# Cross attention in split fp32 on one core: one direct fp32 result unit in batch one in place of two, the softmax sums of batch one folded by accumulating transfers, its order of work written anew, and ten warming products

## The chip, the cores and the metric

The kernel runs on one core of a Trainium2 chip. The metric is device time in microseconds from the start of the program to its end; the median of several runs is compared. A core has five engines that each take their instructions in order: PE (matrix products), ACT (ScalarE), DVE (VectorE), POOL (GpSimd) and SP (SyncE, which here only issues transfers). They wait for each other through semaphores. PE writes to PSUM, ACT and DVE read it; everything else lies in SBUF, 128 partitions wide.

## The reference

Eight batches of cross attention, B = 8, C1 = C2 = 512 channels, N = 1024 positions, D = 64:

```python
q = jnp.einsum('bcn,dc->bnd', x1, Wq) + bq
k = jnp.einsum('bcn,dc->bdn', x2, Wk) + bk[:, None]
v = jnp.einsum('bcn,dc->bdn', x2, Wv) + bv[:, None]
attn = jax.nn.softmax(jnp.einsum('bnd,bdm->bnm', q, k), axis=2)
attn_out = jnp.einsum('bcm,bnm->bcn', v, attn)
return attn_out + x1
```

All of it is fp32, and the inputs are laid out on the host so that channels or positions stand on partitions.

## The kernel before, in words

**Products.** A product of two fp32 operands can be done directly, as PE's fp32 matmul, or in three passes of a faster type (fp32r) on operands that were split. Of an operand a, h is a rounded (`wh`, `xh`, `vh`, `H`), l is the rest (`wl`, `xl`, `vl`, `l`) and d = h - T l, with T = 4096 (`wd`, `xd`, `vd`, `d`). The passes with h and l go to one PSUM bank, X, the pass with d to another, Y, and (T + 1) X - Y gives the product, up to scale and sign. The splitting is work for ACT (h) and DVE (l and d).

**Stages of a batch.** `Q` and `K` project x1 and x2 with the small weights (eight direct products each, 16 rows in the trace); `qe`, `ke` evacuate them on ACT, `qd`, `kc` copy each half to the other 64 partitions by DMA from SP's queue, `qr`, `kr` round them on ACT and `ql`, `kl` make the low halves on DVE. V is made for eight blocks j of 128 positions: `VX.j` and `VY.j` (split, 8 and 4 products), after `sy.j` has put the bias as a seed into Y's bank; `cy.j` on ACT takes Y out and `jn.j` on DVE joins X and Y to `v4`, two blocks to a pair p; `vh.p`, `vl.p`, `vd.p` split the pair again. In batch one the blocks 0 to 2 are direct products instead (`VF.j.c`, four each, joined by `jf.j`). The scores are `S.h.i`: half h (512 queries) and key block i, two products each (with kh and kl against qa), copied out of PSUM by `Sc.h.i` on ACT.

**Softmax and result.** The queries stand in quarters Q of 256 and units u of 128. `F.Q` takes the maximum of a quarter over the key blocks on DVE (four operations), `T.Q` takes it over partitions on POOL, `L.u` subtracts it on DVE, `E.u` is the exponential on ACT, `H.u`, `l.u`, `d.u` split the unit. The result of a unit is `R.u.m`, m = 0 to 7: three split products for each pair of key block and unit, 24 for a unit. In batch one, units 0 and 1 are direct products instead (`RF.u.m`, 8 for a unit, from the unsplit exponentials and v4); they need no H, l and d, and `of.u` evacuates them. Elsewhere `oy.u` on ACT takes Y out with its share of the denominator, and `o.u` on DVE joins it with X. `oa.u` adds x1 by an accumulating DMA from HBM in POOL's queue, `st.u` stores.

**The denominators.** `es.Q` copies half of a quarter's exponentials on ACT, `a1.Q` adds the other half by an accumulating DMA (512 KB) in POOL's queue, `a2.Q` and `a3.Q` fold four columns to two and two to one on DVE (`join`), `tot.Q` sums over partitions on POOL, `few.Q` turns the row into a column with two tiny copies on SP, `rec.Q` is the reciprocal on DVE, and `r2.Q` scales it on ACT. `of`, `oy` and `o` need it.

**Order.** Every engine's order is the order of the words in three lists, written out by hand: `FIRST` for batch one, `MIDDLE` for the six batches between, `LAST`. A word with + belongs to the next batch: its loads (`ldx1`, `ldx2`), Q, K and first scores run inside this one. A scheduler adds the waits and nothing else. PSUM has eight banks: three X, three Y and two for scores ("sc"), handed out in turn; batch one's scores with odd i take a Y bank, and Q and K use the score banks too. Before all that, `begin` issues the first loads and lets PE multiply zeros, nine times, in banks of Y.

Of the kernel before, what the change touches and what calls it, by code (L numbers as in the profile page):

```python
# [27 lines left out]


FIRST = """  # L30
wh.0 VF.0.0 VF.1.0 wl.0 VF.0.1 VF.1.1 wd.0 w4.0 wh.1 VF.0.2 VF.1.2 wl.1 VF.0.3 wd.1 w4.1 ldx2.0 lwq VF.2.0
xh.1 VF.2.1 xl.1 VF.2.2 xd.1 VF.2.3 ldx2.1 lsd xh.2 xh.3 bv xl.2 xl.3 jf.0 jf.2 xd.2 xd.3 sy.3 sy.4 sy.5 K ke
VF.1.3 jf.1 vh.0 vl.0 vd.0 ldx1.0 VY.3 cy.3 ldx1.1 Q kc qe kr qd kl VY.4 cy.4 VX.4 jn.4 VX.3 jn.3 qr ql VY.5
cy.5 VX.5 jn.5 vh.1 vl.1 VX.6 S.0.0 Sc.0.0 S.0.1 Sc.0.1 S.0.2 Sc.0.2 S.0.3 Sc.0.3 S.0.4 Sc.0.4 S.0.5 Sc.0.5
vd.1 S.0.7 +ldx1.1 S.0.6 Sc.0.6 Sc.0.7 F.0 T.0 vh.2 vl.2 +ldx1.0 S.1.1 L.0 F.1 sy.6 L.1 S.1.0 Sc.1.0 Sc.1.1
vd.2 +Q +qe +ldx2.1 S.1.2 Sc.1.2 VY.6 cy.6 jn.6 S.1.3 Sc.1.3 S.1.4 Sc.1.4 S.1.5 Sc.1.5 T.1 L.3 S.1.6 Sc.1.6
VX.7 S.1.7 sy.7 VY.7 E.0 RF.0.0 RF.0.1 RF.0.2 RF.0.3 RF.0.4 RF.0.5 E.1 es.0 RF.1.0 a1.0 L.2 Sc.1.7 F.2 T.2
RF.1.1 E.3 H.3 l.3 a2.0 RF.1.2 RF.1.3 E.2 H.2 es.1 l.2 a1.1 a3.0 +qd +qr +ql RF.1.4 cy.7 jn.7 vh.3 +ldx2.0 +K
+ke RF.1.5 L.5 E.5 RF.0.6 L.4 E.4 H.4 RF.1.6 d.2 RF.0.7 RF.1.7 R.2.0 vl.3 tot.0 few.0 rec.0 r2.0 of.1 oa.1 F.3
of.0 d.3 es.2 R.2.1 R.2.2 R.2.3 R.2.4 R.2.5 R.3.0 R.3.1 R.3.2 R.3.3 R.3.4 a2.1 a3.1 +kc +kr +kl +S.0.0 +S.0.2  # L40
+Sc.0.0 H.5 l.4 R.3.5 st.1 +S.0.1 +Sc.0.1 +Sc.0.2 vd.3 R.2.6 R.3.6 T.3 L.6 L.7 E.7 +S.0.3 +Sc.0.3 R.2.7 R.3.7
d.4 R.4.0 R.4.1 a1.2 a2.2 +S.0.4 +S.0.5 tot.1 few.1 rec.1 oa.0 st.0 a3.2 l.5 d.5 E.6 H.6 l.6 d.6 tot.2 few.2
r2.1 oy.2 oy.3 o.2 o.3 oa.2 oa.3 st.2 st.3 H.7 l.7 rec.2 +Sc.0.4 +Sc.0.5 R.4.2 R.4.3 R.4.4 R.4.5 R.4.6 R.4.7
+S.0.6 +Sc.0.6 d.7 +S.0.7 +Sc.0.7 +F.0 es.3 a1.3 r2.2 oy.4 o.4 oa.4 st.4 +xh.0 +xl.0 +xd.0 +xh.1 +xl.1 R.5.0
R.5.1 R.5.2 R.5.3 R.5.4 R.5.5 R.5.6 R.5.7 oy.5 o.5 +T.0 +L.0 +L.1 +E.0 +E.1 +es.0 oa.5 st.5 a2.3 a3.3 +F.1
+xd.1 R.6.0 R.6.1 R.6.2 R.6.3 R.6.4 R.6.5 R.6.6 R.6.7 oy.6 o.6 +S.1.0 +xh.2 +xl.2 +xd.2 +sy.0 R.7.0 R.7.1
R.7.2 R.7.3 +xh.3 +xl.3 tot.3 few.3 rec.3 +sy.1 +Sc.1.0 +S.1.1 +Sc.1.1 R.7.4 R.7.5 R.7.6 R.7.7 oy.7 o.7
"""
# [34 lines left out]
def kernel(  # L83
# [47 lines left out]
    def bank(tag, name):  # L131
        return psum.tile([P, H], F32, tag=tag, name=name, bufs=BUFS[tag])

    class Batch:
# [182 lines left out]

        def join(self, Q, g):
            es = self.es[Q]
            nc.vector.tensor_tensor(es[:, 0:g, :], es[:, 0:g, :], es[:, g : 2 * g, :], ALU.add)  # L320
# [203 lines left out]
    def begin():  # L524
        for c in range(CT):
            states[0].hx(c)
            states[0].hw(c)
# [2 lines left out]
        nc.vector.memset(spark, 0.0)  # L530

        for i, times in enumerate((3, 3, 3)):
            ps = bank("Y", f"ps_warm{i}")
            for k in range(times):
                nc.tensor.matmul(  # L535
                    ps, warm, warm.unsqueeze(1).to_broadcast([P, 4, P]), start=(k == 0), stop=(k == times - 1)
                )
# [48 lines left out]
```

## Time and profile before

| | |
|---|---|
| median of 3 runs | 659.82 us |
| lowest and highest | 659.54 and 661.53 us |
| the profiled execution | 659.74 us, of which the span of its instructions is 657.9 |
| accumulating and other transfers from POOL (q0) | 13536 packets, 33.04 MB, 30.1% of 16 engines |
| transfers from SP and ACT (q1) | 27168 packets, 56.14 MB, 25.7% of 16 engines |
| HBM | 51.91 MB read, 16.78 MB written |

Times in a row of a timeline are the start in us from the span's start, then the duration in us; a row may merge equal instructions that follow each other (x9). Each direct product of PE stands as two rows. A matmul's duration is longer than its step to the next one, because matmuls are pipelined: what PE can do in a time is read from starts. Words in brackets tell how long the engine sat idle and what ended that.

### The profile page before, as it was taken

What the parts mean: (1) busy time and instruction counts of PE and PEld (TensorE: products, weight loads), DVE (VectorE), ACT (ScalarE), POOL (GpSimd) and SP (SyncE); (2) the same over time, 40 slices, a digit from 0 to 9 for tenths busy, and PEclk for the clock granted to TensorE, in tenths of its full rate; (3) what the DMA queues carried; (4) which work ended last, traced back from release to release, by engine and by line L of the source; (5) the groups of instructions that cost most, each with busy time, mean ns of one, the idle gap of its engine ahead of it and who ended that gap; (6) DMA issues with size and microseconds to landing.
All of it is one profiled execution on the core that took longest, in us unless ns stands there. A gap on an engine that the chain in (4) does not pass through costs nothing.

```text
span 657.9 us, 8049 instructions
## 1 busy us (share of the span) xinstructions
PE 652.4 (99%) x2797; PEld 491.6 (75%) x2797; DVE 615.3 (94%) x689; ACT 451.0 (69%) x668; POOL 204.6 (31%) x162
## 2 busy tenths in 40 slices
PE   9999999999999999999999999999999999999997
PEld 3664888668886688866888668886688776887786
DVE  5789999999999999999999999999999999989994
ACT  5597748767587675875767767687675975759541
POOL 0024532423314343033520335221352214412451
PEclk9999999999999999999999999999999999999999
DMA  8544466564656556374563746737467274642374
GB/s 312 197 143 85 96 134 185 102 187 90 143 152 148 140 115 167 104 200 108 117 173 90 210 96 121 170 83 220 81 128 185 73 206 100 124 113 48 64 137 136
DMA packets 41464, 90.21 MB, mean 137 GB/s; under 512 B 13136, under 2 KB 13904, under 8 KB 37712
## 3 DMA queue, kind: packets, MB, share of 16 engines
q0 software_dynamic: 13536, 33.04, 30.1%
q1 hardware_dynamic: 27168, 56.14, 25.7%
q10 hardware_dynamic: 720, 0.53, 0.2%
q8 instruction: 22, 0.36, 0.2%
q14 instruction: 18, 0.15, 0.1%
HBM read 51.91 MB, written 16.78 MB: 104 GB/s over the span
## 4 chain that ended last, share of the span: by engine, by line
PE 94%; DVE 3%; ACT 2%; issue 0%; DVEq 0%; ACTq 0%
PE ps_oX L435 33%; PE ps_oY L435 17%; PE ps_vX L395 15%; PE ps_s L263 8%; PE ps_vY L395 8%; PE ps_k L206 4%; PE ps_q L206 4%; PE ps_o L460 2%; PE ps_v L375 2%; PE ps_warm L535 1%; DVE vd L427 1%; DVE vl L422 0%; DVE v L413 0%; ACT ps_vY L391 0%; DVE ed L307 0%; DVE e L291 0%
## 5 line engine op out<-in xcount | busy, mean ns | idle before, releaser
L435 PE MATMUL ps_oY<-vd,ed 128*128 128x512 f32 x496 | 193.8, 393 | 0.2 <-DVE ed L307 0.2
L435 PE MATMUL ps_oX<-vh,eh 128*128 128x512 f32 x496 | 193.0, 389 | 0.0
L435 PE MATMUL ps_oX<-vl,el 128*128 128x512 f32 x496 | 193.0, 389 | 0.0
L435 PEld LDWEIGHTS ps_oY<-vd,ed 128*128 128x128 f32 x496 | 93.1, 188 | 25.1 <-issue 5.3
L515 POOL DMA_DIRECT2D o<-in_x1T_dram x62 | 55.6, 917 | 172.2 <-ACT o L512 100.0
L435 PEld LDWEIGHTS ps_oX<-vl,el 128*128 128x128 f32 x496 | 93.0, 188 | 20.2
L435 PEld LDWEIGHTS ps_oX<-vh,eh 128*128 128x128 f32 x496 | 93.1, 188 | 19.5 <-DVE v L413 0.3
L294 ACT ACTIVATE e<-e 128x1024 f32<-128x1024 f32 x64 | 67.7, 1061 | 54.7 <-DVE e L291 53.6
L268 ACT COPY e<-ps_s 128x512 f32<-128x512 f32 x128 | 71.0, 591 | 32.7 <-PE ps_s L263 31.8
L330 POOL PARTITION_ALL_REDUCE den<-es x32 | 82.1, 2565 | 23.3 <-DVE es L320 20.2
L316 POOL DMA_DIRECT2D es<-e x32 | 28.6, 894 | 181.7 <-ACT es L313 172.3
L307 DVE SCALAR_TENSOR_TENSOR ed<-el,eh 128x1024 fp32r<-128x1024 f32 x62 | 81.9, 1321 | 2.1
L302 DVE TENSOR_TENSOR el<-e,eh 128x1024 fp32r<-128x1024 f32 x62 | 79.7, 1302 | 0.0
L291 DVE TENSOR_TENSOR e<-e,top 128x1024 f32<-128x1024 f32 x64 | 76.1, 1220 | 1.0 <-POOL top L283 1.0
L283 POOL PARTITION_ALL_REDUCE top<-max x32 | 46.8, 1463 | 65.3 <-DVE max L279 65.2
L395 PE MATMUL ps_vX<-wh,xh 128*128 128x512 f32 x244 | 66.1, 393 | 0.0
L395 PE MATMUL ps_vX<-wl,xl 128*128 128x512 f32 x244 | 65.2, 389 | 0.0
L395 PE MATMUL ps_vY<-wd,xd 128*128 128x512 f32 x244 | 64.7, 392 | 0.4 <-ACT ps_vY L391 0.4
L298 ACT ACTIVATE eh<-e 128x1024 fp32r<-128x1024 f32 x62 | 64.7, 1055 | 0.5
L410 ACT COPY vy<-ps_vY 128x512 f32<-128x512 f32 x61 | 36.0, 592 | 37.5 <-PE ps_vY L395 37.3
L395 PEld LDWEIGHTS ps_vX<-wh,xh 128*128 128x128 f32 x244 | 45.3, 188 | 14.3 <-DVE max L278 4.1
L395 PEld LDWEIGHTS ps_vY<-wd,xd 128*128 128x128 f32 x244 | 45.5, 188 | 11.8 <-issue 1.3
(59 smaller groups left out, 963.3 us busy)
## 6 DMA issues: line engine op xcount, KB each, us to landing
x<-in_x_dram SPq DMA_DIRECT2D x29, 1024.0 KB, 7.0
es<-e POOLq DMA_DIRECT2D x32, 512.0 KB, 4.9
out_dram<-o SPq DMA_DIRECT2D x63, 256.0 KB, 2.4
o<-in_x1T_dram POOLq DMA_DIRECT2D x62, 256.0 KB, 4.2
x<-in_x_dram SPq DMA_DIRECT2D x5, 512.0 KB, 10.4
k<-k SPq DMA_DIRECT2D x16, 128.0 KB, 2.3
q<-q SPq DMA_DIRECT2D x16, 128.0 KB, 2.4
w_raw<-in_wvT_dram SPq DMA_DIRECT2D x4, 256.0 KB, 3.7
```

What stands on the lines that cost most here:

```text
L206: nc.tensor.matmul(ps[r, :], wqk_sb[:, which, c, :], x(h, c), start=(c == 0), stop=(c == CT - 1))
L263: nc.tensor.matmul(ps, k[:, ts(i, P)], self.qa[:, ts(h, H)], start=(z == 0), stop=(z == 1))
L268: nc.scalar.copy(self.half[h][:, :, i, :], self.ps[h, i].rearrange("p (q n) -> p q n", q=2))
L291: nc.vector.tensor_tensor(e, e, top, ALU.subtract)
L294: nc.scalar.activation(self.unit(u), self.unit(u), AF.Exp)
L298: nc.scalar.activation(self.e[u]["h"], self.unit(u), AF.Copy, scale=SPLIT)
L302: nc.vector.tensor_tensor(self.e[u]["l"], self.unit(u), f32(self.e[u]["h"]), ALU.subtract)
L307: nc.vector.scalar_tensor_tensor(e["d"], f32(e["l"]), -T, f32(e["h"]), ALU.mult, ALU.add)
L330: nc.gpsimd.partition_all_reduce(self.den[Q], self.es[Q][:, 0, :], P, ReduceOp.add)
L395: nc.tensor.matmul(ps, self.c[j // 2][z][:, c, ts(j % 2, P)], w[z][:, c, :], start=(start and c == 0), stop=(stop and c == CT - 1), skip_g ...
L435: nc.tensor.matmul(ps, self.e[u][z][:, m, :], self.v[m // 2][z][:, m % 2, :], start=start, stop=stop, skip_group_check=True,)
L515: nc.gpsimd.dma_start(self.o[u], x1T[self.b, ts(u, P), :], accum_op=ALU.add)
```

## The change

It does four things. `FIRST` lists the words in another order; unit 1's eight `RF.1.m` and `of.1` are replaced by `H.1`, `l.1`, `d.1`, `R.1.m`, `oy.1` and `o.1`. In batch one `join` (a2 and a3 of all four quarters) becomes an accumulating DMA in POOL's queue, from SBUF to SBUF, of 256 and 128 KB. `begin` makes ten warming products. `MIDDLE` and `LAST` stay as they are.

```diff
 FIRST = """
-wh.0 VF.0.0 VF.1.0 wl.0 VF.0.1 VF.1.1 wd.0 w4.0 wh.1 VF.0.2 VF.1.2 wl.1 VF.0.3 wd.1 w4.1 ldx2.0 lwq VF.2.0
...
+wh.0 VF.0.0 VF.1.0 wl.0 VF.0.1 VF.1.1 wd.0 w4.0 wh.1 VF.1.2 wl.1 VF.1.3 wd.1 w4.1 VF.0.2 VF.0.3 ldx2.0 lwq
...
         def join(self, Q, g):
             es = self.es[Q]
+            if self.first:
+                nc.gpsimd.dma_start(es[:, 0:g, :], es[:, g : 2 * g, :], accum_op=ALU.add)
+                return
             nc.vector.tensor_tensor(es[:, 0:g, :], es[:, 0:g, :], es[:, g : 2 * g, :], ALU.add)
...
-        for i, times in enumerate((3, 3, 3)):
+        for i, times in enumerate((4, 3, 3)):
             ps = bank("Y", f"ps_warm{i}")
```

Three lines more in `join` shift the line numbers behind it by three. What the new order does is seen on the engines.

ACT, from the seed's scaling to the rounding of q (`qa`) in batch one, before (names: `bv_seed` the bias, `ps_vY` a seeded Y bank, `k`, `q` the projections, `vy` a Y bank taken out):

```order
L184 ACTIVATE bv_seed<-bv_seed 128x512
L391 COPY ps_vY_3_153<-bv_seed 128x512
L391 COPY ps_vY_4_155<-bv_seed 128x512
L391 COPY ps_vY_5_157<-bv_seed 128x512
L213 ACTIVATE k_168<-ps_k_159,bqk_sb 64x512 x2
L417 ACTIVATE vh_0_173<-v_0_0_145 128x1024
L410 COPY vy_3_187<-ps_vY_3_153 128x512
L213 ACTIVATE q_204<-ps_q_193,bqk_sb 64x512 x2
L252 ACTIVATE kh_207<-k_168 128x1024
L410 COPY vy_4_217<-ps_vY_4_155 128x512
L236 ACTIVATE qa_240<-q_204 128x1024
```

and with the change, from the evacuation of k; the next two rows are `vy_5` and `qa`:

```order
L213 ACTIVATE k_148<-ps_k_137,bqk_sb 64x512 x2
L361 ACTIVATE xh_2_155<-x_0_1_135 128x1024
L184 ACTIVATE bv_seed<-bv_seed 128x512
L394 COPY ps_vY_3_175<-bv_seed 128x512
L394 COPY ps_vY_4_177<-bv_seed 128x512
L394 COPY ps_vY_5_179<-bv_seed 128x512
L213 ACTIVATE q_201<-ps_q_182,bqk_sb 64x512 x2
L252 ACTIVATE kh_204<-k_148 128x1024
L413 COPY vy_3_206<-ps_vY_3_175 128x512
L413 COPY vy_4_208<-ps_vY_4_177 128x512
L420 ACTIVATE vh_0_210<-v_0_0_171 128x1024
L420 ACTIVATE vh_1_224<-v_0_1_173 128x1024
```

The evacuation of k now stands ahead of xh of block pair 2, the scaling of the bias and the three seed copies, and all of these ahead of q; two vh stand ahead of qa where one `vy` stood.

PE, the work behind the next batch's Q in batch one, before (`ps_s_1_i` scores of the second half, `ps_vX`, `ps_vY` V):

```order
L263 MATMUL ps_s_1_2_356<-qa_240,kh_207 128x512
L263 MATMUL ps_s_1_2_356<-qa_240,kl_211 128x512
L395 MATMUL ps_vY_6_331<-wd,xd_3_151 128x512 x4
L263 MATMUL ps_s_1_3_368<-qa_240,kh_207 128x512
L263 MATMUL ps_s_1_3_368<-qa_240,kl_211 128x512
L263 MATMUL ps_s_1_4_372<-qa_240,kh_207 128x512
L263 MATMUL ps_s_1_4_372<-qa_240,kl_211 128x512
L263 MATMUL ps_s_1_5_376<-qa_240,kh_207 128x512
L263 MATMUL ps_s_1_5_376<-qa_240,kl_211 128x512
L263 MATMUL ps_s_1_6_383<-qa_240,kh_207 128x512
L263 MATMUL ps_s_1_6_383<-qa_240,kl_211 128x512
L395 MATMUL ps_vX_7_387<-wh,xh_3_138 128x512 x4
```

and with the change, where two scores (`ps_s_1_0`, `ps_s_1_5`) precede these rows behind Q:

```order
L263 MATMUL ps_s_1_4_327<-qa_256,kh_204 128x512
L263 MATMUL ps_s_1_4_327<-qa_256,kl_212 128x512
L398 MATMUL ps_vX_6_351<-wh,xh_3_146 128x512 x4
L398 MATMUL ps_vX_6_351<-wl,xl_3_151 128x512 x4
L398 MATMUL ps_vX_7_360<-wh,xh_3_146 128x512 x4
L398 MATMUL ps_vX_7_360<-wl,xl_3_151 128x512 x4
L398 MATMUL ps_vY_6_317<-wd,xd_3_153 128x512 x4
L263 MATMUL ps_s_1_3_385<-qa_256,kh_204 128x512
L263 MATMUL ps_s_1_3_385<-qa_256,kl_212 128x512
L263 MATMUL ps_s_1_2_392<-qa_256,kh_204 128x512
L263 MATMUL ps_s_1_2_392<-qa_256,kl_212 128x512
L263 MATMUL ps_s_1_1_395<-qa_256,kh_204 128x512
```

V's blocks 6 and 7 now stand between the scores of the second half. On SP, earlier, batch two's first 1 MB load (`ldx1.1`) has moved ahead of batch one's two copies of q (`qd`).

DVE, from the first reciprocal to the low half of batch two's k (`kl`), before (`es` the two joins, `ed`, `el` splits of a unit, `max` a quarter's maximum):

```order
L339 RECIPROCAL r_0_496<-few_0_493 128x2
L276 TENSOR_TENSOR max_3_503<-e_1_337 128x512
L278 TENSOR_TENSOR max_3_503<-max_3_503,e_1_337 128x512 x2
L279 TENSOR_TENSOR max_3_503<-max_3_503 128x256
L307 SCALAR_TENSOR_TENSOR ed_3_510<-el_3_432,eh_3_430 128x1024
L320 TENSOR_TENSOR es_1_440<-es_1_440 128x512
L320 TENSOR_TENSOR es_1_440<-es_1_440 128x256
L256 TENSOR_TENSOR kl_552<-k_468,kh_550 128x1024
L302 TENSOR_TENSOR el_4_564<-e_1_337,eh_4_477 128x1024
L427 TENSOR_TENSOR vd_3_575<-vh_3_455,vl_3_489 128x1024
```

and with the change:

```order
L342 RECIPROCAL r_0_532<-few_0_485 128x2
L276 TENSOR_TENSOR max_3_549<-e_1_322 128x512
L278 TENSOR_TENSOR max_3_549<-max_3_549,e_1_322 128x512 x2
L279 TENSOR_TENSOR max_3_549<-max_3_549 128x256
L425 SCALAR_TENSOR_TENSOR vl_3_563<-vh_3_452,v_0_3_379 128x1024
L430 TENSOR_TENSOR vd_3_565<-vh_3_452,vl_3_563 128x1024
L256 TENSOR_TENSOR kl_576<-k_477,kh_574 128x1024
L302 TENSOR_TENSOR el_4_592<-e_1_322,eh_4_539 128x1024
```

The joins are gone, and both `vl` and `vd` of the last pair of V now stand directly ahead of `kl`; `vd` stood behind it.

More of the change, by code (lines that the diff above doesn't have):

```diff
@@ L30 @@
 FIRST = """
-wh.0 VF.0.0 VF.1.0 wl.0 VF.0.1 VF.1.1 wd.0 w4.0 wh.1 VF.0.2 VF.1.2 wl.1 VF.0.3 wd.1 w4.1 ldx2.0 lwq VF.2.0
[L32 to L45, printed above, removed]
@@ L46 @@
-+xd.1 R.6.0 R.6.1 R.6.2 R.6.3 R.6.4 R.6.5 R.6.6 R.6.7 oy.6 o.6 +S.1.0 +xh.2 +xl.2 +xd.2 +sy.0 R.7.0 R.7.1
-R.7.2 R.7.3 +xh.3 +xl.3 tot.3 few.3 rec.3 +sy.1 +Sc.1.0 +S.1.1 +Sc.1.1 R.7.4 R.7.5 R.7.6 R.7.7 oy.7 o.7
+wh.0 VF.0.0 VF.1.0 wl.0 VF.0.1 VF.1.1 wd.0 w4.0 wh.1 VF.1.2 wl.1 VF.1.3 wd.1 w4.1 VF.0.2 VF.0.3 ldx2.0 lwq
+VF.2.0 xh.1 VF.2.1 xl.1 VF.2.2 xd.1 VF.2.3 ldx2.1 K xh.3 ke xl.3 xd.3 xh.2 xl.2 xd.2 lsd ldx1.0 bv ldx1.1 jf.0
+jf.2 sy.3 sy.4 sy.5 jf.1 Q kc VY.3 VY.4 qe kr cy.3 cy.4 vh.0 kl VX.3 jn.3 vh.1 vl.1 VY.5 cy.5 VX.5 +ldx1.1
@@ new lines @@
+VX.4 qd qr ql S.0.0 S.0.1 S.0.2 S.0.3 Sc.0.0 Sc.0.1 Sc.0.2 Sc.0.3 S.0.4 Sc.0.4 vl.0 vd.0 S.0.5 Sc.0.5 S.0.6
+Sc.0.6 vd.1 S.0.7 Sc.0.7 +ldx1.0 +Q +qe F.0 sy.6 S.1.0 Sc.1.0 S.1.5 S.1.4 jn.4 jn.5 vh.2 T.0 L.0 L.1 E.0 E.1
+H.1 es.0 a1.0 F.1 VX.6 VX.7 l.1 d.1 VY.6 cy.6 jn.6 T.1 L.2 L.3 S.1.3 +ldx2.1 a2.0 a3.0 S.1.2 S.1.1 Sc.1.1
+Sc.1.2 Sc.1.3 Sc.1.4 Sc.1.5 vl.2 E.2 H.2 l.2 RF.0.0 RF.0.1 RF.0.2 RF.0.3 RF.0.4 RF.0.5 vd.2 sy.7 S.1.6 Sc.1.6
+S.1.7 Sc.1.7 E.3 es.1 a1.1 F.2 T.2 +qd +qr +ql VY.7 cy.7 jn.7 vh.3 d.2 R.1.0 L.5 H.3 l.3 +ldx2.0 +K +ke R.1.1
@@ new lines @@
+tot.0 few.0 R.1.2 RF.0.6 R.1.3 R.1.4 a2.1 a3.1 RF.0.7 R.1.5 R.2.0 E.5 L.4 E.4 es.2 a1.2 d.3 R.2.1 R.2.2 R.2.3
+R.2.4 R.2.5 rec.0 r2.0 of.0 oa.0 H.4 R.3.0 R.3.1 F.3 R.3.2 R.3.3 R.3.4 vl.3 vd.3 H.5 R.1.6 +kc +kr +kl +S.0.0
++S.0.1 +Sc.0.0 +Sc.0.1 R.1.7 oy.1 l.4 d.4 +S.0.2 R.3.5 +Sc.0.2 +S.0.3 +Sc.0.3 T.3 L.6 L.7 E.6 o.1 tot.1 few.1
+rec.1 r2.1 R.2.6 R.3.6 +S.0.5 a2.2 a3.2 +S.0.4 +Sc.0.4 +Sc.0.5 R.2.7 R.3.7 oy.3 R.4.0 R.4.1 st.0 oa.1 st.1 l.5
+d.5 oy.2 o.2 oa.2 st.2 o.3 oa.3 H.6 l.6 d.6 +xh.0 +xl.0 +xd.0 +S.0.7 R.4.2 R.4.3 R.4.4 R.4.5 R.4.6 R.4.7 tot.2
@@ L48 @@
+few.2 E.7 H.7 es.3 l.7 a1.3 d.7 a2.3 rec.2 +S.0.6 +Sc.0.6 +Sc.0.7 +F.0 r2.2 oy.4 o.4 oa.4 st.4 +xh.2 +xl.2
+R.5.0 R.5.1 R.5.2 R.5.3 R.5.4 R.5.5 R.5.6 R.5.7 oy.5 o.5 R.6.0 R.6.1 R.6.2 R.6.3 R.6.4 R.6.5 R.6.6 R.6.7 oy.6
++sy.0 st.3 +S.1.1 +T.0 +L.0 +L.1 +E.0 +E.1 +F.1 +xh.1 +xl.1 +xd.1 o.6 +xh.3 +xl.3 +S.1.0 R.7.0 R.7.1 R.7.2
+R.7.3 +Sc.1.0 +Sc.1.1 +es.0 +sy.1 +xd.2 a3.3 tot.3 few.3 rec.3 oa.5 st.5 R.7.4 R.7.5 R.7.6 R.7.7 oy.7 o.7
 """
```

## Prediction

> **What bounds the kernel now.** I read the page's busy times and its chain of waits first, then who waits for whom on PE in the first 115 us, then the timelines of PE, ACT, DVE and POOL over the stretch that the change rewrites.
>
> ```profile
> span 657.9 us, 8049 instructions
> PE 652.4 (99%) x2797; PEld 491.6 (75%) x2797; DVE 615.3 (94%) x689; ACT 451.0 (69%) x668; POOL 204.6 (31%) x162
> PE 94%; DVE 3%; ACT 2%; issue 0%; DVEq 0%; ACTq 0%
> ...
> PE ps_warm L535 <- DVE spark L530: 1.0, 1, 1.0
> ```
>
> PE sets the time: it carries 94% of the chain and is idle for 657.9 - 652.4 = 5.5 us. The last line is the whole list of PE's waits up to 115 us: after the first microsecond PE never stands still in the first batch. So the change can win only PE work that it removes, and each wait that it makes costs in full. DVE at 94% is the engine with the least room behind PE.
>
> ```profile
> 0.98 3.88 PE L535 MATMUL ps_warm<-warm 128*128 128x512 bf16 x9 [0.98 <-DVE spark L530]
> 4.70 9.61 PE L375 MATMUL ps_v<-w_raw,x 128*128 128x512 f32 x22
> 14.23 3.65 PE L206 MATMUL ps_k<-x,wqk_sb 128*64 128x512 f32 x16
> 17.82 1.12 PE L375 MATMUL ps_v<-w_raw,x 128*128 128x512 f32 x2
> ...
> 32.59 0.39 PE L263 MATMUL ps_s<-qa,kh 128*128 128x512 f32 x1
> ...
> 40.80 0.50 PE L263 MATMUL ps_s<-qa,kh 128*128 128x512 f32 x1
> ...
> 47.28 9.61 PE L460 MATMUL ps_o<-v,e 128*128 128x512 f32 x22
> 56.82 3.65 PE L206 MATMUL ps_k<-x,wqk_sb 128*64 128x512 f32 x16
> ...
> 65.73 0.39 PE L435 MATMUL ps_oX<-vh,eh 128*128 128x512 f32 x1
> ...
> 72.08 0.39 PE L435 MATMUL ps_oX<-vl,el 128*128 128x512 f32 x1
> ```
>
> Starts give PE's prices. A direct fp32 product stands as two rows: (56.82 - 47.28) / 11 = 0.867 us. A split product: the rows from 65.73 to 72.08 are 29 starts in a row, so 6.35 / 28 = 0.227 us. A projection of q or k: 17.82 - 14.23 = 3.59 us. Each change between the two kinds costs about 0.1 us (the first score after q, at 40.80, takes 0.50 where others take 0.39).
>
> **The change part by part.** *Unit 1's result* loses 8 direct products, 8 x 0.867 = 6.93 us, and gains 24 split ones, 24 x 0.227 = 5.44 us: **-1.49 us** on PE. It also brings H.1, l.1, d.1, oy.1 and o.1 to ACT and DVE, off PE's path but in its queues.
>
> *The tenth warming product.* Nine take 4.70 - 0.98 = 3.72 us, 0.413 each; direct products run at full pace from 4.70 on, with no wait of PE for the input. The tenth delays them by 0.21 us (half of 0.413, if the pace has doubled by then) to 0.41. I take **+0.2**, since the next row is at full pace. [...]
>
> *The order up to the first score.* All 12 direct value products, then K, then Q now stand in a row, so PE would reach S.0.0 after 4.9 + 12 x 0.867 + 2 x 3.59 + 0.1 + 36 x 0.227 = 30.7 us (the 36: VY.3, VY.4, VX.3, VY.5, VX.5, VX.4). But ACT:
>
> ```profile
> 13.27 2.00 ACT L358 ACTIVATE xh<-x 128x1024 fp32r<-128x1024 f32 x2 [0.78 <-DMA x<-in_x_dram]
> 15.36 0.63 ACT L184 ACTIVATE bv_seed<-bv_seed 128x512 f32<-128x512 f32 x1
> 16.02 1.63 ACT L391 COPY ps_vY<-bv_seed 128x512 f32<-128x512 f32 x3
> 17.93 1.39 ACT L213 ACTIVATE k<-ps_k,bqk_sb 64x512 f32<-64x512 f32 x2 [0.29 <-PE ps_k L206]
> 20.82 1.06 ACT L417 ACTIVATE vh<-v 128x1024 fp32r<-128x1024 f32 x1 [1.50 <-DVE v L387]
> 24.92 1.06 ACT L252 ACTIVATE kh<-k 128x1024 fp32r<-128x1024 f32 x1
> 26.00 0.59 ACT L410 COPY vy<-ps_vY 128x512 f32<-128x512 f32 x1
> 27.71 1.06 ACT L236 ACTIVATE qa<-q 128x1024 fp32r<-128x1024 f32 x1 [1.11 <-DMA q<-q]
> ...
> 28.98 1.22 DVE L239 TENSOR_TENSOR qa<-q,qa 64x1024 fp32r<-64x1024 f32 x1
> ```
>
> K's evacuation ke now stands ahead of xh.2, the seed's scaling and the three seed copies, and K ends at 4.9 + 10.4 + 3.6 = 18.9. From there ACT runs without a break: ke starts 0.1 later (17.93 after 17.82) and takes 1.39; xh.2 1.0; bv 0.66; three copies 1.63; qe 1.39; kh 1.0; two vy 1.0; two vh 2.0; vy 0.5; qa 1.06: it ends at 30.5. DVE's low half of qa adds 1.22, and 0.15 passes to PE: S.0.0 at **31.9**. In the trace it started at 32.59 with VX.6 (8 x 0.227 = 1.8 us) ahead of it. The loss against PE's own 30.7 is **+1.1**, part of it already at VY.3, which waits for its seed copy. From both sides: 0.7, if back-to-back ACT instructions overlap a little more; 2, if the q copy lands late (a rival).
>
> *The scores of batch one's second half.* S.0.0 to S.0.7 take 16 x 0.227 = 3.6 and batch two's Q 3.7: it ends at 39.2. S.1.4 now stands third behind it and takes the very PSUM bank that Q used, so it waits for qe.
>
> ```profile
> 40.95 1.40 ACT L213 ACTIVATE q<-ps_q,bqk_sb 64x512 f32<-64x512 f32 x2 [1.01 <-PE ps_q L206]
> ...
> 45.95 2.00 ACT L294 ACTIVATE e<-e 128x1024 f32<-128x1024 f32 x2
> 47.98 1.05 ACT L313 COPY es<-e 128x1024 f32<-128x1024 f32 x1
> ...
> 50.50 1.06 ACT L298 ACTIVATE eh<-e 128x1024 fp32r<-128x1024 f32 x1
> ```
>
> qe started 0.15 after Q's end (40.95 against 40.80) and takes 1.40: 40.75, and S.1.4 at 40.9. PE, with only four products between (0.9) and 0.1 of switching, is there at 40.2: **+0.7** (0.5 to 0.8). S.1.1 then needs the bank of VY.6, which cy.6 frees. cy.6 now stands on ACT behind qe, sy.6 0.52, a score copy 0.5, vh.2 1.0, two E 2.05, H.1 1.0, es.0 0.95: its 0.59 end at 47.3, S.1.1 at 47.4. PE: 40.9 + 0.45 + 20 x 0.227 + 0.9 = 46.8. **+0.6** (0.4 to 0.8).
>
> *The first score of batch two.* From 47.4 PE has six direct products (5.2), S.1.6, S.1.7 and VY.7 (1.8), seven triples of R.1 and eleven of R.2 and R.3 (54 x 0.227 = 12.3), two more direct products and K with their switching (5.9), and S.1.1 itself and one product (0.7): it is at S.0.0 of batch two, at the product with kl, at about 73.2.
>
> ```profile
> 68.88 1.22 DVE L256 TENSOR_TENSOR kl<-k,kh 128x1024 fp32r<-128x1024 f32 x1
> 70.01 2.12 DVE L302 TENSOR_TENSOR el<-e,eh 128x1024 fp32r<-128x1024 f32 x1
> ...
> 64.03 1.42 DVE L278 TENSOR_TENSOR max<-max,e 128x512 f32<-128x512 f32 x2
> ...
> L320 DVE TENSOR_TENSOR es<-es x64: 411/550/1544, 54.5 to 638.4; 128x512 f32<-128x512 f32 x32, 128x256 f32<-128x256 f32 x32
> ...
> 69.06 2.69 POOL L330 PARTITION_ALL_REDUCE den<-es  x1
> ```
>
> kl ended at 70.1. DVE starts its chain 0.7 earlier, with the first score; it has l.1, d.1 and vd.3 more ahead of kl (3 x 1.13, the step from 68.88 to 70.01) and four joins less (4 x 0.55: 2.2), and I estimate 2 us of waits that it did not have: l.1 for H.1, which ACT ends at 45.8, about 1.1, the rest for ql and for pairs that feed each other. That gives 72.6. The rows of L302 and L330 show what a reduction on POOL does to DVE: 2.12 us instead of 1.22. Quarter 1's reduction now falls there: 73.5 to 74.2. **+0.8** (0 to 1.1). The 0.2 to 0.4 us of switching around the lone direct products vanish in this wait.
>
> *The joins.* Eight DVE instructions become accumulating copies of 256 and 128 KB in POOL's queue.
>
> ```profile
> x<-in_x_dram SPq DMA_DIRECT2D x29, 1024.0 KB, 7.0
> es<-e POOLq DMA_DIRECT2D x32, 512.0 KB, 4.9
> o<-in_x1T_dram POOLq DMA_DIRECT2D x62, 256.0 KB, 4.2
> q<-q SPq DMA_DIRECT2D x16, 128.0 KB, 2.4
> few<-den SPq DMA_DIRECT2D x64, 0.5 KB, 2.7
> ...
> DMA to landing us min/median/max: 4.5/4.9/6.7
> ```
>
> (The last line is es alone.) Such a copy of 256 or 128 KB from SBUF to SBUF is in no row: between 2.4 (a plain copy of 128 KB) and 6.7 (the slowest es). I take 4.2 for both, the row of the same kind and size. Quarter 0: es.0 ends at 46.7, a1 4.9, a2 and a3 8.4 with 0.1 of waiting each, reduction 2.7, the two few copies 3.3: 66.2. rec.0, which reads them, comes up on DVE at about 66.5: kl's end at 72.6, less kl, vd.3 and vl.3 (3.5) and F.3 (three operations of 0.7 and a half one, 2.6). So DVE saves 2 us and nothing waits, by a margin of 0.3 only; behind rec.0 in DVE's queue stand F.3, vl.3, vd.3 and kl. I take **+0.4** for the quarters where it fails. [...]
>
> Sum: -1.5 + 0.2 + 1.1 + 0.7 + 0.6 + 0.8 + 0.4 = **+2.3 us**. Later batches run the same list as before and keep the shift. The profiled execution took 659.74 us (span 657.9 and 1.8 around it), 0.08 under the median of 659.82; 659.74 + 2.3 = 662.0, and 662.1 against the median.
>
> **The rivals.**
>
> *Nothing new waits* (14%). If ACT and DVE keep ahead as they do in the trace, only PE's own work counts: -1.5 + 0.2, **658.5**; with half of the waits 660.3. For it: PE has no wait at all now, and ACT is at 69%. Against: three of the waits follow from a fixed order of long instructions on one engine and need no luck to occur. This is the case that ends within measurement of no change or better.
>
> *The joins come late* (17%). It decides from a2 + a3 = 8.7 us on. At 5.5 each, between the median and the slowest es, quarter 0's rec.0 comes 2.3 us late and holds DVE, hence vd.3 and kl; quarter 2 does the same through r2.2 and oy.4: about +4 on the sum, **666**. For it: POOL's queue is in order, and a2 and a3 wait there for landings ahead of the maxima's reductions. Against: the copies are half and a quarter of es.
>
> *q's copy behind a load* (8%).
>
> ```profile
> 24.21 1.62 SPq L220 DMA_DIRECT2D q<-q  x2
> 25.93 1.01 SPq L150 DMA_DIRECT2D x<-in_x_dram  x2
> ```
>
> SP now issues batch two's 1 MB load ahead of q's copies, at about 21.0. If its 7.0 us run first, it ends at 28.0 and the copies 2.4 later, at 30.4; qa could start at 29.5: +1.0, **663.1**. For it: same queue. Against: the load should be mostly done when the copies are issued at 24.4.
>
> **How the numbers follow.** The forecast has 58%, the rivals 14, 17 and 8, and 3 are left for what I do not see. About 0.3% (2.0 us) is what a measurement of this kernel tells from no change: 657.8 to 661.8. The low ends of the terms added up give +0.3, the high ones about +3.4, so the forecast's own range is 660.0 to 663.2, four fifths of it lie above 661.8, 46%, with both late rivals 71% slower. Within 0.3%: 12 + 13 = 25%; faster 4%, since even without a wait the gain is 1.3 us and only a shorter last batch could add to it. The range from 660.0 to 666 holds eight of ten.
>
> **What would show it.** In the profile after: ps_o stands with 16 rows (now 32), ps_v starts at about 4.9, the first score at 31.9, batch two's first at 74, and PE waits on ACT at ps_s (two, 0.5 to 0.8 each), on DVE at the first score and at batch two's first (0.5 to 1.1). If PE's list of waits stays empty up to 115 us, I am wrong by the waits; if POOL's den waits long for es<-es landings and DVE's reciprocal for few, the joins are late.

## The result, and the profile after

The changed kernel takes **666.85 us** (median of four runs, 666.23 to 667.51) against 659.97 (659.54 to 661.53) for the kernel before on the same chip: a ratio of 1.0096, 95% interval 1.0084 to 1.0108. It is slower by 6.9 us of the medians, 6.3 by the ratio. The forecast was 662.1 with a range of 660 to 666. The sign was right, the size was not. The span of the profiled execution is 665.7, 7.8 more than before.

PE's list of waits of the changed kernel, from 4 to 116 us (which product waited, for whom, us in all, how often, the longest). Before, the same list had no wait between 1 and 115 us.

```profile
PE ps_vX L398 <- DVE o L503: 2.2, 1, 2.2
PE ps_s L263 <- DVE kl L256: 0.8, 1, 0.8
PE ps_s L263 <- ACT vy L413: 0.4, 1, 0.4
PE ps_s L263 <- ACT q L213: 0.4, 1, 0.4
PE ps_vY L398 <- DVE xd L371: 0.3, 1, 0.3
PE ps_vY L398 <- ACT ps_vY L394: 0.3, 1, 0.3
PE ps_s L263 <- DVE qa L239: 0.2, 1, 0.2
PE ps_oY L438 <- DVE vd L430: 0.2, 1, 0.2
```

The six from the second line on stand at the places that the forecast named. The last, for vd of batch one's last pair (vd.3), is not among them, and neither is the first, which is by far the longest. That one stands in batch two's V (VX.1, which needs the X bank that o.6 of batch one gives back), at 109 to 111 us, and it has a successor that no list of waits shows. The changed kernel by stretches of two us; after the stretch come its length and the busy time of PE, PEld, DVE, ACT and POOL, then the clock granted to PE, the DMA share and GB/s:

```profile
108.00:110.00 2.00, 0.98 (x5) 0.47 (x3) 1.97 (x3) 2.00 (x4) 0.09 (x1) 1.00 0.73 96
110.00:112.00 2.00, 0.83 (x4) 0.71 (x5) 2.00 (x3) 1.42 (x4) 1.83 (x2) 1.00 0.63 108
112.00:114.00 2.00, 2.00 (x8) 1.55 (x7) 2.00 (x4) 0.80 (x2) 0.00 (x0) 0.65 1.04 198
114.00:116.00 2.00, 2.00 (x6) 1.62 (x5) 2.00 (x4) 0.51 (x2) 0.00 (x0) 0.50 1.03 321
116.00:118.00 2.00, 2.00 (x10) 1.63 (x10) 2.00 (x3) 2.00 (x4) 0.00 (x0) 1.00 1.02 422
```

PE stands still for about 2.2 us; then it is busy without a gap, but the 14 products from 111.17 to 116.07 take 4.9 us where 0.227 for each would make 3.2, and the granted clock is 0.65 and 0.50. Lost at that clock: 2 x 0.35 + 2 x 0.50 = 1.7 us. Wait and slow stretch make 3.9 of the 7.8 us. The first product of VX.0, just ahead of the wait, starts 4.0 us later than before (107.00 against 102.98), the first of VY.2, behind the slow stretch, 8.1 later (116.07 against 107.97).

Who is late? Backwards from that wait. The product, and o.6 on DVE:

```profile
111.17 1.20 PE L398 MATMUL ps_vX<-wh,xh 128*128 128x512 f32 x4 [2.19 <-DVE o L503]
...
110.43 0.68 DVE L503 SCALAR_TENSOR_TENSOR o<-ps_oX,oy 128x512 f32<-128x512 f32 x1
...
92.38 1.23 DVE L307 SCALAR_TENSOR_TENSOR ed<-el,eh 128x1024 fp32r<-128x1024 f32 x1
96.56 0.17 DVE L342 RECIPROCAL r<-few 128x2 f32<-128x2 f32 x1 [2.96 <-DMA few<-den]
```

From 96.56 to 110.43 DVE has only one gap, of 0.6; before that stands the reciprocal of quarter 2 (rec.2), for which DVE was idle 2.96 us. It waits for the two few copies. They stand on SP behind a store, and that store behind an accumulating transfer of o; den, which they copy, stands on POOL behind the transfers of o for tiles 1 to 3:

```profile
85.26 4.77 SPq L522 DMA_DIRECT2D out_dram<-o  x2
90.13 1.87 SPq L338 DMA_DIRECT2D few<-den  x2
...
75.16 0.92 POOL L321 DMA_DIRECT2D es<-es  x1
79.58 0.86 POOL L321 DMA_DIRECT2D es<-es  x1 [3.50 <-DMA es<-es]
81.36 0.87 POOL L518 DMA_DIRECT2D o<-in_x1T_dram  x1 [0.92 <-DVE r L342]
84.83 1.76 POOL L518 DMA_DIRECT2D o<-in_x1T_dram  x2 [2.59 <-DVE o L503]
86.06 2.30 POOL L333 PARTITION_ALL_REDUCE den<-es  x1
88.91 0.90 POOL L316 DMA_DIRECT2D es<-e  x1 [0.55 <-ACT es L313]
```

Both joins of quarter 2 have landed at 82.3. The reduction could have begun then; it begins at 86.06, behind two transfers that themselves wait for DVE. It ends at 88.4, few is issued at 90.13, and it takes 6.4 us until the reciprocal runs, with the 512 KB of the next quarter's es issued 1.2 us ahead of it. In the kernel before, the reduction of quarter 2 began at 77.90, ahead of o's transfers on POOL (84.33), few was issued at 80.55, 9.6 us earlier than now (of which PE's own lateness at the wait is 4.0), and rec.2 ran at 85.74 without a wait:

```profile
77.90 2.62 POOL L330 PARTITION_ALL_REDUCE den<-es  x1 [5.36 <-DVE es L320]
...
80.55 1.12 SPq L335 DMA_DIRECT2D few<-den  x2
...
85.74 0.16 DVE L339 RECIPROCAL r<-few 128x2 f32<-128x2 f32 x1
```

The two places come from the lists, not from the joins. Before, `tot.2 few.2` stood ahead of `oa.2 oa.3 st.2 st.3`; in the new order they stand behind `st.1`, `oa.2` and `oa.3`.

The joins themselves were faster than forecast. Of the eight transfers, from issue to landing:

```profile
DMA to landing us min/median/max: 2.7/3.3/4.1
```

That is 3.3 to 4.1 for the 256 KB and 2.7 to 3.8 for the 128 KB, 7.1 for the pair of quarter 0, 6.8 for that of quarter 2.

### The profile page after: what moved, and what is told of

It is laid out like the page before. It is cut to its first block, busy times and chain, and to the rows that moved or that the text cites. A ratio compares the mean times of both kernels' runs of the same rounds, so it can differ in the third digit from the quotient of the medians.

```text
span 665.7 us, 8070 instructions
## 1 busy us (share of the span) xinstructions
PE 655.4 (98%) x2806; PEld 494.5 (74%) x2806; DVE 615.3 (92%) x684; ACT 451.9 (68%) x669; POOL 205.7 (31%) x170
## 4 chain that ended last, share of the span: by engine, by line
PE 79%; DVE 4%; ACT 1%; issue 0%; DVEq 0%; DMA 0%; ACTq 0%
PE ps_oX L438 29%; PE ps_oY L438 15%; PE ps_vX L398 14%; PE ps_vY L398 7%; PE ps_s L263 7%; PE ps_k L206 3%; PE ps_q L206 3%; DVE e L291 1%; DVE max L278 1%; DVE vd L430 1%; DVE vl L425 0%; DVE v L416 0%; DVE ed L307 0%; ACT eh L298 0%; ACT e L294 0%
## 5 line engine op out<-in xcount | busy, mean ns | idle before, releaser
L438 PE MATMUL ps_oY<-vd,ed 128*128 128x512 f32 x504 | 197.5, 394 | 0.3 <-DVE ed L307 0.2
L438 PE MATMUL ps_oX<-vh,eh 128*128 128x512 f32 x504 | 196.2, 389 | 0.0
L438 PE MATMUL ps_oX<-vl,el 128*128 128x512 f32 x504 | 196.1, 389 | 0.0
L438 PEld LDWEIGHTS ps_oY<-vd,ed 128*128 128x128 f32 x504 | 94.6, 188 | 26.9 <-issue 6.3
L438 PEld LDWEIGHTS ps_oX<-vl,el 128*128 128x128 f32 x504 | 94.5, 188 | 20.6
L438 PEld LDWEIGHTS ps_oX<-vh,eh 128*128 128x128 f32 x504 | 94.6, 188 | 20.0 <-issue 0.5
L307 DVE SCALAR_TENSOR_TENSOR ed<-el,eh 128x1024 fp32r<-128x1024 f32 x63 | 83.5, 1326 | 2.6 <-DVE el L302 0.5
L283 POOL PARTITION_ALL_REDUCE top<-max x32 | 42.7, 1334 | 57.7 <-DVE max L279 57.6
```

Source lines behind the costliest of these rows:

```text
L283: nc.gpsimd.partition_all_reduce(self.top[Q], self.fold[Q][:, 0, :], P, ReduceOp.max)
L307: nc.vector.scalar_tensor_tensor(e["d"], f32(e["l"]), -T, f32(e["h"]), ALU.mult, ALU.add)
L438: nc.tensor.matmul(ps, self.e[u][z][:, m, :], self.v[m // 2][z][:, m % 2, :], start=start, stop=stop, skip_group_check=True,)
```

## The experiments

Ratios are to the kernel before, run beside each group on the same chip, with 95% intervals. The groups ran on different chips, so runs of different groups are compared by these ratios.

**Joins back on DVE.** In `join`, the branch for batch one is taken out:

```diff
-            if self.first:
-                nc.gpsimd.dma_start(es[:, 0:g, :], es[:, g : 2 * g, :], accum_op=ALU.add)
-                return
             nc.vector.tensor_tensor(es[:, 0:g, :], es[:, 0:g, :], es[:, g : 2 * g, :], ALU.add)
```

> The changed kernel with batch one's eight joins back on DVE, all else as changed. Theory (late joins): the transfers make quarter 2's sums late, DVE idles 2.96 us at the reciprocal that waits for few, and the V product of batch two waits 2.2 us for a bank and then runs at half clock; with DVE joins that reciprocal waits under 0.5 us, PE has no wait on o, and the time falls by about 4.1, to 662.7 (661.5 to 663.5). Rival (the new order itself puts o.6 too late on DVE, whoever adds): the wait on o stays over 1.5 us and the time at 665.5 to 668.

Measured: 674.82, ratio 1.0211 (1.0195 to 1.0226), 14 us above the kernel before and 8 above the change. Both expected times fell. PE's waits between 60 and 125 us:

```profile
PE ps_vX L395 <- DVE o L500: 7.3, 2, 5.4
PE ps_oX L435 <- ACT o L473: 1.6, 1, 1.6
```

and in DVE's timeline the last join and the reciprocal behind it:

```profile
113.98 0.42 DVE L320 TENSOR_TENSOR es<-es 128x256 f32<-128x256 f32 x1
120.72 0.17 DVE L339 RECIPROCAL r<-few 128x2 f32<-128x2 f32 x1 [6.32 <-DMA few<-den]
```

The list places quarter 3's last join right ahead of its reduction. For a transfer that place is a place in POOL's queue. For a DVE instruction it is one behind the splitting of batch two's x, 12 us later than the transfer was issued (102.20), and reduction, few and reciprocal follow it. That makes the second wait for o, of 5.4 us. The first, of 1.9 us, stands at VX.1 as in the change, although quarter 2's joins are on DVE here and end at 83.1. Its reduction on POOL again begins behind o's transfers, as the new list has it:

```profile
87.69 2.30 POOL L330 PARTITION_ALL_REDUCE den<-es  x1
...
111.85 1.19 PE L395 MATMUL ps_vX<-wh,xh 128*128 128x512 f32 x4 [1.88 <-DVE o L500]
```

So the wait at VX.1 belongs to the new order, whoever adds: the rival had that, though not the time. What the transfers cost as such this run does not show, since quarter 3's place in the list was made for them.

**The old order with transfers.** The kernel before, with that branch put into `join`; a2 and a3 keep the places they had.

> The kernel before, its order and nine products kept, with batch one's eight joins as accumulating transfers. Theory (late joins): quarter 0's reciprocal, which had 1.0 us to spare after few landed, waits 3 to 5 us on DVE, and the time grows by 3 to 6, to 663 to 666. Rival (the transfers relieve DVE of 4.4 us and are harmless; the cost of the change is its order): 659.3 to 660.4.

Measured: 676.09, ratio 1.0237 (1.0222 to 1.0252). The theory had the sign and the place, not the size: DVE waits three times for few, not once, and two waits of PE are of 5 and 3 us (DVE's list of waits, then PE's).

```profile
DVE r L342 <- DMA few<-den: 20.0, 3, 8.3
...
PE ps_s L263 <- ACT e L268: 4.9, 1, 4.9
PE ps_vX L398 <- DVE o L503: 2.9, 1, 2.9
```

The new order without the transfers costs 14 us, the transfers without the new order 15, both together 6.9. The two cannot be priced apart in this way.

**Quarter 2's reduction early.** Order of batch one alone, two words moved:

```diff
-... R.4.1 st.0 oa.1 st.1 l.5 d.5 oy.2 o.2 oa.2 st.2 o.3 oa.3 ... R.4.7 tot.2 few.2 E.7 ...
+... R.4.1 st.0 oa.1 tot.2 few.2 st.1 l.5 d.5 oy.2 o.2 oa.2 st.2 o.3 oa.3 ... R.4.7 E.7 ...
```

> The changed kernel, joins still transfers; quarter 2's reduction and its two few copies stand ahead of o's transfers of tiles 2 and 3 on POOL and of the store of tile 1 on SP. Theory (late joins, by way of the two queues): den of quarter 2 starts at about 82.3 in place of 86.1, few lands before 88 in place of 96.3, the reciprocal does not wait, and the time falls by about 4, to 662.8 (661.5 to 664). Rival (the transfers of 256 and 128 KB crowd the DMA engines, so few lands late wherever it is issued): few still takes over 5 us to land and the time stays at 665 to 667.

Measured: **662.54**, ratio 1.0027 (1.0017 to 1.0036). Its reduction on POOL, its few on SP and its reciprocal on DVE:

```profile
81.42 2.73 POOL L334 PARTITION_ALL_REDUCE den<-es  x1 [0.22 <-DMA es<-es]
...
84.17 1.11 SPq L339 DMA_DIRECT2D few<-den  x2
...
91.32 0.16 DVE L343 RECIPROCAL r<-few 128x2 f32<-128x2 f32 x1
```

The reduction now waits for the join alone, the reciprocal for nothing, PE's wait on o is gone and the clock stays at 1.00. Joins, transfers and their sizes are the same as in the change. This settles the cause of the larger part of the loss (4.6 of 6.3 us, by the ratios): not the transfers, but the places that the new list gave quarter 2's reduction and copies in the queues of POOL and SP. Which of the two places weighs more was not tested.

**VY.1 ahead of VX.1 in batch two.** The change, and for the second batch alone the two words swapped.

> The changed kernel with VY.1 ahead of VX.1 on PE in batch two alone, nothing else. VY.1's four products (0.9 us) then stand in the 2.2 us in which PE waits for o.6. Theory (PE's idle time of over 2 us makes the clock fall to half for about 4 us, some 1.9 us of work): idle time falls to 1.3, no stretch at half clock follows, and the time falls by 2.5 to 3, to about 664. Rival (the half clock comes whenever PE waits there, or by the phase of the clock's check): 0.9 less, about 666, with a granted clock of 0.5 to 0.65 between 112 and 116 us as before.

Measured: 665.59, ratio 1.0069 (1.0055 to 1.0083), against 1.0096 for the change: 1.8 us less, by the ratios. PE's idle stretch became 1.2 us (VY.1 now waits for its seed), VX.1 behind it does not wait for o.6, and in the two stretches where the change had 0.65 and 0.50 the clock column now reads 1.00:

```profile
112.00:114.00 2.00, 2.00 (x10) 1.66 (x9) 2.00 (x4) 0.78 (x2) 0.00 (x0) 1.00 1.04 197
114.00:116.00 2.00, 2.00 (x10) 1.56 (x10) 2.00 (x4) 1.58 (x3) 0.00 (x0) 1.00 1.00 315
```

Of the 2.6 us that this saves there (0.9 of idle time, 1.7 of clock), two new waits at 122 and 123 us for ACT's copies, 0.5 and 0.4 with PE's restart, take 0.9 back. The shorter idle stretch, which begins at the same time as in the change (109.0), brought no slow one, as the theory had it; the time is between the two expectations.

**Nine warming products** in the change.

> The changed kernel with nine warming products in place of ten. Theory (the tenth product costs its own 0.43 us and no more; the slow first V products of the profile belong to the phase of the clock in that execution): 666.4 (666.0 to 666.7), and the first V products run 0.43 or 0.85 us each by chance. Rival (a tenth product shifts the work against the clock's full-speed point, so that 1.0 us of V at half speed comes with it): 665.4, V at 0.43 a pass from 4.7 on.

Measured: 666.10, ratio 1.0080 (1.0068 to 1.0092). That is about 1 us under the change, but the two intervals overlap, and its profile had a slow start too (up to 20 us PE has 53 instructions, in the change 52, with the early reduction 56); open.

**The small waits, one by one.** Three repairs on top of the early reduction, each a few words of the list, then all together.

```diff
 seeds
-K xh.3 ke xl.3 xd.3 xh.2 xl.2 xd.2 lsd ldx1.0 bv ldx1.1 jf.0 jf.2 sy.3 sy.4 sy.5 jf.1 Q kc
+K xh.3 xl.3 xd.3 xh.2 xl.2 xd.2 lsd ldx1.0 bv ldx1.1 jf.0 jf.2 sy.3 sy.4 sy.5 jf.1 ke Q kc
 banks
-S.1.5 S.1.4 jn.4 ... H.1 es.0 a1.0 F.1 VX.6 VX.7 l.1 d.1 VY.6 cy.6 jn.6 T.1
+S.1.5 jn.4 ... H.1 F.1 VX.6 S.1.4 VX.7 l.1 d.1 VY.6 cy.6 es.0 a1.0 jn.6 T.1
 kl
-H.4 R.3.0 R.3.1 F.3 R.3.2 R.3.3 R.3.4 vl.3 vd.3 H.5 R.1.6 +kc +kr +kl ... T.3 L.6 L.7 E.6 o.1 tot.1 few.1
+H.4 +kc +kr R.3.0 R.3.1 R.3.2 R.3.3 R.3.4 vl.3 vd.3 F.3 H.5 R.1.6 +kl ... tot.1 few.1 T.3 L.6 L.7 E.6 o.1
```

> Quarter 2's early reduction, as in the run of that name, and in addition the bias seed's scaling and three seed copies on ACT ahead of K's evacuation (as in the kernel before). Theory (the waits of the new order add up one by one on PE): the two waits of VY.3 and VY.4 for the seed, 0.47 + 0.52 with their switching, go, the wait of the first score stays under 0.6, and the time falls by 0.7 to 1.0 against the run with the early reduction alone. Rival (the waits stand in one chain and the next one swallows what the first gives back): the first score then waits 1.2 or more and the time is within 0.3 of that run.

> Early reduction, and score 1.4 behind VX.6 on PE, and cy.6 ahead of es.0 on ACT. Theory (one by one): the waits of scores 1.4 and 1.1 for their PSUM banks (0.56 each, 0.11 of restart each) fall to 0 to 0.2 and the time falls by 0.9 to 1.3. Rival (one chain): batch two's first score waits for kl by as much more (1.0 now, then 2.0) and the time is within 0.4 of the run with the early reduction alone.

> Early reduction, and quarter 3's maxima on DVE behind vl.3 and vd.3, quarter 1's reduction on POOL ahead of quarter 3's maximum, kh on ACT ahead of eh of unit 5. Theory (one by one): vd.3 no longer holds PE (0.3 to 0.6) and kl is free of the reduction's stretch, so the first score of batch two waits under 0.3 for it in place of 1.0: the time falls by 0.8 to 1.4. Rival (DVE's total work decides, its order does not): kl ends as late as before, the wait stays near 1.0 and the time within 0.3.

> All three repairs and the early reduction together. Theory (one by one): no wait over 0.5 us on PE between 5 and 110 us, the sum of the three gains, 2.4 to 3.6 less than with the early reduction alone: 0.9 to 1.6 us below the kernel before. Rival (one chain, DVE's or ACT's work decides): the waits come back later on PE, and the time is within 0.5 of the kernel before or above it.

Measured: 661.94, ratio 1.0023 (1.0013 to 1.0034); 663.28, 1.0042 (1.0030 to 1.0055); 662.19, 1.0023 (1.0013 to 1.0033); all together 662.60, 1.0034 (1.0021 to 1.0046). None is told apart from the early reduction alone at 1.0027, except that the banks repair may be worse. Each repair did take away the wait it aimed at or shorten it, and the next one grew, as the rivals had it: with the seeds and xh early the first score waits 0.6 for qa in place of 0.2; with the banks repaired VY.7 waits for its seed; with kl's repair vd.3 no longer holds PE, but kl is as late as it was. PE's waits with all three:

```profile
PE ps_s L263 <- DVE kl L256: 0.9, 1, 0.9
PE ps_vY L398 <- ACT ps_vY L394: 0.5, 1, 0.5
PE ps_s L263 <- DVE qa L239: 0.5, 1, 0.5
```

**The chain run.** Those three waits and score 1.1's, each taken at its place: `+kl` ahead of `F.3`, `sy.7` ahead of `vl.2 E.2`, `qd` ahead of `+ldx1.1` and `vh.1 vl.1` behind `qr ql`, `VX.7` behind `VY.6`. Then the same with nine warming products, with all joins on DVE (a3.3 behind a2.3, tot.3 and few.3 behind batch two's E.1), with quarter 0's joins alone on DVE (`if self.first and Q:`), and with `o.1` ahead of `L.6 L.7`.

> The run with all repairs, and the four waits that its profile still shows taken at their places: kl on DVE ahead of quarter 3's maxima (first score of batch two waited 1.1), sy.7 ahead of exp of unit 2 on ACT (VY.7, 0.67), q's copies ahead of the load on SP and qa ahead of vh.1 on ACT (first score, 0.61), VY.6 ahead of VX.7 on PE (score 1.1, 0.30). Theory (each wait is one instruction that stands in the wrong place of a queue): PE waits less than 0.8 us in all between 5 and 110 us and the time falls by about 2.5 against the run with all repairs, to 659 to 660.5, at or below the kernel before. Rival (DVE, full from 47 to 75 us, is the bound there): kl's wait of about 1 us shows up at another product and the time stays within 0.8 of that run, above the kernel before.

> The same with nine warming products. Theory (a product at half clock costs half its time against V work that would run at half clock too): 0.2 less, not told apart by the times; V starts 0.43 earlier. Rival (ten are needed): 0.5 to 1 us more, with V's first products at 0.85 us in this profile and in most runs.

Measured: 661.45, ratio 1.0010 (1.0001 to 1.0019), and with nine products 661.04, ratio 1.0008 (0.9999 to 1.0017). The four waits are off the list; from 4 to 116 us the first of the two has left

```profile
PE ps_oX L438 <- ACT o L476: 0.8, 1, 0.8
PE ps_oX L438 <- DVE o L503: 0.3, 1, 0.3
```

so the first theory holds for the waits, and the rival for the time: a new wait of 0.8 stands where none over 0.2 was, at unit 3's bank, which of.0 gives back after rec.0. The gain over the run with all repairs is 1.6 of the 2.5 expected (1.0034 to 1.0010, on two chips). Nine or ten products are not told apart.

> The chain run with batch one's joins on DVE, quarter 3's last join right behind the one before it and its reduction behind batch two's second exp. Theory (between 47 and 75 us DVE has no room for the four joins of quarters 0 and 1, 2.3 us in all): kl ends about 2 us later, batch two's first score waits 1.5 to 2.5 for it, and the time is 1.5 to 3 above the chain run. Rival (the transfers' latency costs as much as DVE's time): within 0.7 of the chain run or below.

> The chain run with nine warming products, and quarter 0's two joins on DVE, those of quarters 1 to 3 as transfers. Theory (what is left of the loss is quarter 0's join latency: two copies one after the other put its reciprocal, hence the scaling copy that frees the bank of unit 3's sums, 0.95 late on PE): the reciprocal of quarter 0 stands ready some 4 us earlier, that wait falls under 0.3, and the time falls by 0.5 to 1.0, to 659.8 to 660.6. Rival (DVE, full from 47 to 75 us, gives the time for the joins back): that wait or one for kl or ed stays at 0.9 or more and the time is within 0.3 or above.

> The same, and unit 1's output on DVE ahead of the two subtractions of units 6 and 7, which took 2.35 in front of it while PE waited 0.49 for its bank. Theory: a further 0.3 to 0.5 less, 659.4 to 660.2, a ratio to the kernel before of 0.998 to 0.9995. Rival: PE then waits for ed of unit 4 or 5 or for exp of unit 6 and nothing is gained.

> The chain run with nine warming products and unit 1's output ahead of those two subtractions, all joins as transfers. Theory (the waits of units 3 and 4 are separate): the wait at unit 3 stays at 0.9 to 1.0, the one at unit 4 goes, 0.3 to 0.5 less than the chain run. Rival (one chain): no change.

Measured: all joins on DVE 669.34, ratio 1.0130 (1.0116 to 1.0144), 8 us above the chain run. Neither expectation has that: no product waits for kl, but PE waits 2.8 us for o at VX.1, and 1.4 and 1.6 for quarter 0's reciprocal and output, with a stretch at half clock behind these two. Quarter 0's alone 663.03, 1.0044 (1.0032 to 1.0057); with o.1 early 663.06, 1.0042 (1.0028 to 1.0055); o.1 early and all joins transfers 661.57, 1.0018 (1.0009 to 1.0027). My theory for quarter 0 fell. With its joins on DVE, on POOL and on DVE:

```profile
59.08 2.07 POOL L283 PARTITION_ALL_REDUCE top<-max  x1 [2.31 <-DVE max L279]
61.05 2.68 POOL L333 PARTITION_ALL_REDUCE den<-es  x1
...
68.12 0.17 DVE L342 RECIPROCAL r<-few 128x2 f32<-128x2 f32 x1 [0.60 <-DMA few<-den]
```

The reciprocal still waits 0.6, because den stands behind quarter 2's maximum on POOL, which waits for DVE's maxima, and these have the two joins, 1.15 us, ahead of them. As transfers, in the chain run with nine products, quarter 0's joins landed at 57.6, and its reduction began 1.1 us later, at 58.68, behind the same maximum. So their latency was hidden, and DVE's time was not: PE's wait at unit 3 grew from 0.8 to 1.6. With o.1 early the wait for it goes, and VX.1 waits 1.1 to 1.3 for o.6 in its place; why was not followed. No version beats the kernel before; the best, at 1.0008, is not told from it.

## Why the prediction was wrong, step by step

- **RF.1 to R.1, -1.5.** The program is as expected (ps_o stands with 16 rows). No run measured its worth alone. The run with the early reduction, in which little but the small waits is left, stands 1.8 us above the kernel before, and the sum without the joins was 1.9; but that is luck in part. The spans of the two profiles differ by 2.7 (660.6 and 657.9), and the parts in them come to 3.0: -1.5, 0.3 for V's later start, 4.2 for the small waits.
- **The small waits.** The forecast had +1.1 up to the first score, +0.7 and +0.6 for the two PSUM banks, +0.8 for kl, 3.2 in all. Measured by the gaps between starts of products, with the 0.1 that PE needs to restart (the first product behind a wait takes 0.50 where the next ones take 0.39 or 0.40): 1.4 (VY.3 0.47, VY.4 0.51, the first score 0.44), 0.67, 0.67, and 1.1 with 0.4 for vd.3 ahead of it: 4.2. The places were right but for vd.3, which was not forecast. So were the causes, but for VY.4: it waits for xd, whose xh stands behind K's evacuation on ACT, and not for a seed copy.
- **What stands behind batch two's first score, in the sum only the +0.4 for the joins: this is the step that failed.** The sum has no term for the new places of quarter 2's reduction and few. I followed quarter 0's chain to its end, found 0.3 to spare, and put 0.4 on "the quarters where it fails" without following them. In place of the 0.4 the runs show about 4: 2.2 of wait at VX.1 and 1.7 of half clock behind it. It was not the joins' latency (3.3 in the median where I took 4.2), and not the engine that joins. In quarter 2 the joins end 4.6 us later than DVE's did (82.3 against 77.7), but with joins on DVE the wait at VX.1 stays (1.9), and with the transfers kept and two words moved it is gone. The new list puts the reduction behind o's transfers on POOL and few behind a store on SP and beside es: 10.8 us later at the reciprocal (96.56 against 85.74) where PE is 4.0 late. No row of before held a price for that; the two lists held the order.
- **Quarter 0's margin of 0.3** was not there either, and again not by the joins. They landed at 60.9; the reduction began at 61.19, when quarter 2's maximum left POOL, and the second few copy landed 4.3 us after the first was issued, where I took 3.3. The reciprocal waited 0.63, and DVE has no gap from there to kl, so a part of kl's 1.1 comes from this.
- **The late rival, 17%, 666.** It had quarter 2 and POOL's order in it, and its time is 0.85 below the measured one. That nearness is luck: it was to decide from 8.7 us for a pair, and the pairs took about 7. It made the joins late, and what was late stood in the queues behind them.
- **The half clock, 1.7 us.** In no term and no rival. The trace of before has no idle stretch of PE to learn it from (its longest wait behind the start is 0.4), and the sum priced a wait at its length.
- **The tenth product, +0.2.** V starts 0.52 later in the profile (5.22 against 4.70), and its first products ran slower in that execution (seven took 3.95 us), another 0.9 us. That second part is not the tenth product's, as far as the starts in the last section tell: it came with nine products too. The 0.2 or 0.4 for the product itself is not told from nothing by any run.
- **The range** was drawn from bounds on terms, each taken alone. It left out the case that a wait is long enough to bring a second loss with it. One chance has a slip: of a range from 660.0 to 663.2 with its middle at 662.1, not four fifths lie above 661.8 but about half.

## What to carry to other kernels

When an order is written anew, follow every instance of a step that it moves, not the tightest-looking one, through each in-order queue: what matters is which instruction it now stands behind, and that changes by steps of several microseconds (10.8 us at quarter 2's reciprocal). An order written by hand and the engine that a step runs on are one design; the time of a run with one half undone is not the price of the other half, but its waits can still tell whose they are. In the change, PE's idle stretch of 2.2 us cost 3.9, as the granted clock was 0.50 for 3.4 us behind it: look at the clock behind an idle stretch, not at its length alone.
